# Two scores moved beside the attention outputs in a software-pipelined two-layer graph network

## The chip, the cores and the metric

The kernel runs on one core of a Trainium2 chip. Its time is device microseconds for one whole execution; a table entry is the median of several executions. The engines of the core are TensorE (PE in the profile: matmuls, and PEld: the loads of their weights), VectorE (DVE), ScalarE (ACT), GpSimd (POOL) and SyncE (SP, which here only issues DMAs). Each engine works through its own list of instructions strictly in order and waits on semaphores for the others.

## The reference

128 graphs of 128 nodes with 512 features pass two layers. Both start with a layer norm and a relu, and both add their result to x.

```python
# layer 0 (weights Wq, Wk, Wv of 512 x 512)
h = relu(layernorm(x))
q, k, v = h @ Wq.T, h @ Wk.T, h @ Wv.T
rel = adjacency.T * (q @ k.T)          # 128 x 128 for each graph
rel = rel / norm(rel, axis=2)
x = x + rel @ v
# layer 1 (8 heads of 64, with biases)
h = relu(layernorm(x))
q, k, v = h @ Wq + bq, h @ Wk + bk, h @ Wv + bv
scores = q @ k.T / sqrt(64) + (0 where adj else -1e9)
x = x + softmax(scores) @ v
```

All of it is float32.

## The kernel before

The 128 graphs are taken in 32 groups of four. A group passes four stages, and four neighbouring groups are in work at once. In the lists of steps their names are: `f`, the group whose x is being loaded and whose layer norm statistics are taken; `m`, the group in layer 0; `n`, the same group as `m` when its layer 1 starts (`n.stat`, `n.hn`, `n.T`); `l`, the group before, in layer 1; and `p`, the group before that, whose last two attention outputs and whose way back to x are still open. After a cycle each name passes on: `n` becomes `l`, `l` becomes `p`.

Every 512 x 512 product with a group's 512 rows is done in seven quarter products (steps `P1` to `P7`, a Strassen-Winograd scheme). Each is eight matmul passes of 128x256 in a PSUM bank, at line 218, followed by one emptying: a copy by ACT (`Q`, `K`, `G` and layer 0's `V`) or by DVE (layer 1's `V`, line 235), or an addition by DVE (line 242). Banks `x` and `z` are used by several of the seven in turn: `P1`, `P6`, `P7`, `P4` all accumulate in `x`, `P5` and `P3` in `z`. The next of them may not start before the emptying of the one before has read the bank: `Q.P6` waits for the copy of `Q.P1`, `Q.P3` for the copy of `Q.P5`, `Q.P7` for that of `Q.P6`, and `Q.P4` for the addition of `Q.P7`. There are four such banks, so `Q.P5` also waits for the addition of `Q.P2`, which gives a bank back and which needs the copy of `Q.P1`.

Matrices are turned with the help of DRAM. `hn`, `ex` and `oc` on ACT write a tile and send it to a scratch tensor (line 184, ACT's queue, one DMA of 512 KB); `rd`, `wr` and `rdo` fetch it back in blocks (line 192, SP's queue, four DMAs of 128 KB); `T`, `wt` and `ot` on DVE then transpose 32x32 blocks (lines 313, 478, 585). The fetched tiles share one pool of two buffers:

```python
tpool = ctx.enter_context(tc.tile_pool(name="tpool", bufs=2))
...
u = tpool.tile([P, n * TB, 8 * BK // n], F32, tag="u", name=f"u_{name}")
```

A fetch can't be issued before one of the two has been read by its transpose. In the program as built, for both kernels, the fetch `m.rd0` waits for `p.wt3`, and `m.rd1` for the second transpose of `p.ot0`.

Layer 1's attention of graph b is `S` (scores, line 445: 16 matmul passes with 64 rows and 128 columns of the array, eight heads into two PSUM banks of which there is one set), `mk` (DVE: mask added, line 454, and row maxima, line 456), `ex` (ACT: eight exponentials, line 463, and the send), `wr` (fetch), `wt` (DVE: reciprocal and transpose). `A0` and `A1` (line 562: 32 passes each, 128 rows and 64 columns) make the attention outputs of graphs 0, 1 and 2, 3. `oc`, `rdo`, `ot` bring them back: two ACT copies and a send, four fetches, and for each graph a transpose, a scaling (line 590, DVE), the addition to x and the store (lines 597 and 598, POOL).

The order of everything is written by hand, in four lists of steps: `FIRST`, `SECOND` (groups 0 and 1), `ORDER` (30 cycles) and `LAST`. The lists are emitted in turn under a manual schedule, so each engine's order is the order of the list, thinned to what that engine does; a step's instructions on all engines are emitted together. What a step on one engine waits for on another is worked out by the framework. DVE therefore does `p.wt3`, `p.ot0`, the addition of `Q.P3`, `m.T0`, the addition of `Q.P7`, `m.T1` in this sequence, in both kernels.

Of the kernel before, what the change touches and what calls it, by code (L numbers as in the profile page):

```python
# [21 lines left out]
def kernel(  # L22
# [343 lines left out]
    class Layer0(Layer):  # L366
        n = 0
# [54 lines left out]
    class Layer1(Layer):  # L422
        n = 1
# [189 lines left out]
        m.V.P2 l.S1 l.mk1 m.V.P5  # L613
        l.ex1 l.wr1 l.wt0 m.R m.mask_rel m.square f.stat2 f.stat3 f.inv1 m.V.P6 m.V.P3 m.N m.norms l.S2 l.mk2
        m.V.P7 l.ex2 l.wr2 l.wt1 m.O0 m.xO0 m.O1 m.xO1 n.stat0 n.stat1 n.inv0 m.V.P4 n.hn0 n.rd0 l.start_v l.V.P1
        m.O2 m.xO2 m.O3 m.xO3 n.stat2 n.stat3 n.inv1 l.S3 l.mk3 l.V.P2 l.V.P5 n.hn1 l.V.P6 l.wt2 n.rd1 l.ex3
        l.wr3 l.V.P3 l.V.P7 n.T0 l.A0 l.oc0 l.V.P4 n.T1 n.start
    """.split()
    ORDER = """
        l.Q.P1 p.rdo0 l.sumA l.Q.P2 m.hn0 l.sumB l.K.P1 m.rd0 m.hn1 l.K.P2 m.rd1 p.wt3 l.Q.P5  # L620
        p.ot0 l.Q.P6 l.Q.P3 p.A1 p.oc1 p.rdo1 m.T0 l.Q.P7 l.K.P5 m.T1 l.K.P6 l.Q.P4 f.load0 f.load1
        l.K.P3 m.sumA l.K.P7 m.sumB m.start m.G.P1 l.K.P4 m.G.P2 l.S0 l.mk0 m.G.P5 m.G.P6 l.ex0 l.wr0
        p.ot1 m.G.P3 m.V.P1 m.G.P7 f.stat0 f.stat1 f.inv0 m.V.P2 f.load2 f.load3 m.G.P4 l.S1 l.mk1 m.V.P5
        l.ex1 l.wr1 l.wt0 m.R m.mask_rel m.square f.stat2 f.stat3 f.inv1 m.V.P6 m.V.P3 m.N m.norms l.S2 l.mk2
        m.V.P7 l.ex2 l.wr2 l.wt1 m.O0 m.xO0 m.O1 m.xO1 n.stat0 n.stat1 n.inv0 m.V.P4 n.hn0 n.rd0 l.start_v l.V.P1
        m.O2 m.xO2 m.O3 m.xO3 n.stat2 n.stat3 n.inv1 l.S3 l.mk3 l.V.P2 l.V.P5 n.hn1 l.V.P6 l.wt2 n.rd1 l.ex3
        l.wr3 l.V.P3 l.V.P7 n.T0 l.A0 l.oc0 l.V.P4 n.T1 n.start
    """.split()
    LAST = """
        l.Q.P1 p.rdo0 l.sumA l.Q.P2 l.sumB l.K.P1 l.K.P2 p.wt3 l.Q.P5 p.ot0 l.Q.P6 l.Q.P3 l.K.P5 l.K.P6 l.K.P3  # L630
        l.Q.P7 l.S0 l.mk0 l.K.P7 l.Q.P4 l.ex0 l.wr0 l.K.P4 l.S1 l.mk1 p.A1 p.oc1 p.rdo1 l.start_v l.V.P1
        l.ex1 l.V.P2 l.V.P5 l.S2 l.mkA2 l.mkB2 l.V.P6 l.exA2 l.exB2 l.wt0 l.wr1 l.V.P3 l.V.P7 l.S3 l.mkA3 l.mkB3
        l.tw2 l.wt1 l.exA3 l.exB3 l.V.P4 l.An0 l.fin0 l.An1 l.fin1 p.ot1 l.tw3 l.An2 l.fin2 l.An3 l.fin3
# [15 lines left out]
    with tc.manual_schedule(engines={EN.PE, EN.SP, EN.Pool, EN.DVE, EN.Activation}):  # L649
        p, l, m = None, None, Layer0(0)  # L650
# [9 lines left out]
        f = Layer0(1)  # L660
# [7 lines left out]
        for g in range(NG):  # L668
            n = Layer1(g)
            if g:  # L670
                f = Layer0(g + 1) if g + 1 < NG else None
            run((FIRST, SECOND, ORDER)[min(g, 2)], p=p, l=l, m=m, n=n, f=f, w=Weights1())
            p, l, m = l, n, f
# [31 lines left out]
```

## Time and profile before

| | |
|---|---|
| median of 3 runs | 2538.28 us (2534.71 to 2539.89) |
| the profiled execution's own time | 2538.26 us |
| its span, first to last instruction | 2536.5 us |
| PE busy | 2512.7 us (99%) |
| DVE, ACT, POOL busy | 1707.5 (67%), 1023.9 (40%), 535.0 us (21%) |
| one of the 30 cycles, by the repeat of the same matmul | 77.57 us |
| granted TensorE clock, mean | 0.997 |

A busy share is the engine's own; matmuls overlap each other, so PE's share is not a share of its peak. The chain that ended last follows the work back from the last instruction, at each step to what released it. In a view by time, a line gives start and duration in us, the engine (q: its queue), the line of the kernel, the operation, out<-in, the shapes, how many instructions were merged, and in square brackets the idle time before it and what ended it. The scratch tensors are `d_h`, `d_w`, `d_o`; what is fetched from them is `u_h`, `u_w`, `u_o`.

### The profile page before, as it was taken

The page shows a single profiled execution, that of the slowest core. Times are in us where ns is not written, and L with a number is a line of the kernel's source. Part 1 is how long each engine was busy: PE and PEld are TensorE (multiplying, and loading weights), DVE is VectorE, ACT ScalarE, POOL GpSimd, SP SyncE. Part 2 cuts the span into 40 slices and gives each one's busy share as a digit, 9 for nine tenths or more (in the row PEclk, how much of TensorE's full clock was granted, in tenths as well). Part 3 has the DMA queues.
Part 4 walks back from the last instruction along what each step waited for, and adds up shares of the span by engine and source line. Part 5 has one row for each costly group of instructions (what it writes and reads, how often), then busy time and mean ns, then how long its engine had stood idle before and what let it go on. Part 6 is the DMA issues. An engine that isn't in the chain of part 4 may idle for free.

```text
span 2536.5 us, 40820 instructions
## 1 busy us (share of the span) xinstructions
PE 2512.7 (99%) x14672; PEld 2135.8 (84%) x14672; DVE 1707.5 (67%) x2484; ACT 1023.9 (40%) x3248; POOL 535.0 (21%) x945
## 2 busy tenths in 40 slices
PE   8999999999999999999999999999999999999998
PEld 6888888888888888888888888888888888888886
DVE  5566766667676667666677666676666676666765
ACT  2334443444433344434444333444344443334433
POOL 5121212211122212121111222121211112221211
PEclk9999999999999999999999999999999999999999
DMA  5255544555444555445554445554455644455542
GB/s 171 88 179 166 187 145 140 172 170 185 154 145 151 182 167 183 146 146 168 168 188 152 142 155 178 171 182 142 148 169 165 193 151 143 156 176 174 175 133 93
DMA packets 370475, 405.71 MB, mean 160 GB/s; under 512 B 29600, under 2 KB 286752, under 8 KB 370272
## 3 DMA queue, kind: packets, MB, share of 16 engines
q1 hardware_dynamic: 278992, 167.92, 23.4%
q10 hardware_dynamic: 70384, 166.74, 17.8%
q0 software_dynamic: 20896, 68.44, 7.8%
q8 instruction: 115, 1.88, 0.3%
q14 instruction: 88, 0.72, 0.1%
HBM read 204.80 MB, written 198.18 MB: 159 GB/s over the span
## 4 chain that ended last, share of the span: by engine, by line
PE 97%; DVE 1%; DMA 1%; ACT 0%; issue 0%; POOL 0%; SPq 0%; ACTq 0%; DVEq 0%; POOLq 0%
PE pv_x L218 18%; PE pq_x L218 9%; PE pv_z L218 9%; PE pk_x L218 9%; PE pg_x L218 8%; PE pss L445 5%; PE po L562 5%; PE pv_y L218 5%; PE pg_z L218 4%; PE pq_z L218 4%; PE pr L382 4%; PE pk_z L218 4%; PE po L414 4%; PE pk_y L218 2%; PE pg_y L218 2%; PE pq_y L218 2%
## 5 line engine op out<-in xcount | busy, mean ns | idle before, releaser
L463 ACT ACTIVATE e<-pss,nmax 128x128 f32<-128x128 f32 x1008 | 355.0, 380 | 190.9 <-DVE nmax L456 168.5
L597 POOL TENSOR_TENSOR xb<-xb,o 128x512 f32<-128x512 f32 x124 | 158.2, 1276 | 1103.6 <-DVE o L590 976.4
L218 PE MATMUL pv_x<-wc_v,h 128*128 128x256 f32 x1280 | 300.8, 382 | 0.0
L218 PEld LDWEIGHTS pv_x<-wc_v,h 128*128 128x128 f32 x1280 | 240.3, 190 | 51.0 <-DVE v L242 11.7
L301 ACT ACTIVATE hn<-xb,shift,rstd 128x512 f32<-128x512 f32 x252 | 190.9, 807 | 152.4 <-POOL shift L293 152.4
L218 PE MATMUL pv_z<-wc_v,s 128*128 128x256 f32 x1024 | 245.1, 382 | 0.0
L313 DVE STREAM_TRANSPOSE h<-u_h 128x1024 f32<-128x1024 f32 x126 | 156.5, 1242 | 98.9 <-DMA u_h<-d_h 92.0
L463 ACT ACTIVATION_READ_ACCUMULATOR e<-pss,nmax 128x1 f32 x1008 | 221.2, 219 | 0.0
L454 DVE TENSOR_TENSOR pss<-pss,mask 128x1024 f32<-128x1024 f32 x126 | 154.7, 1228 | 96.2 <-PE pss L445 96.2
L218 PEld LDWEIGHTS pv_z<-wc_v,s 128*128 128x128 f32 x1024 | 192.0, 190 | 28.6
L218 PE MATMUL pv_x<-wc_v,s 128*128 128x256 f32 x768 | 184.9, 384 | 0.0
L218 PE MATMUL pq_x<-h,wc_q 128*128 128x256 f32 x768 | 184.7, 383 | 0.0
L283 DVE BATCH_NORM_STATS2 st<-xb 128x6 f32<-128x512 f32 x256 | 172.0, 672 | 16.6 <-DMA xb<-in_x_dram 16.6
L218 PE MATMUL pk_x<-h,wc_k 128*128 128x256 f32 x768 | 181.5, 379 | 0.0
L445 PEld LDWEIGHTS pss<-kT,qT 64*128 64x128 f32 x2048 | 124.6, 188 | 48.7 <-PE po L414 23.5
L290 POOL TENSOR_SCALAR rstd<-mv 128x2 f32<-128x2 f32 x128 | 28.6, 223 | 642.8 <-DVE mv L284 642.7
L218 PEld LDWEIGHTS pq_x<-h,wc_q 128*128 128x128 f32 x768 | 143.4, 190 | 23.5 <-ACT oT L573 5.1
L218 PEld LDWEIGHTS pk_x<-h,wc_k 128*128 128x128 f32 x768 | 145.8, 190 | 19.9
L218 PEld LDWEIGHTS pv_x<-wc_v,s 128*128 128x128 f32 x768 | 140.8, 190 | 20.4
L456 DVE TENSOR_REDUCE nmax<-pss 128x8 f32<-128x1024 f32 x126 | 154.2, 1224 | 4.4
L478 DVE STREAM_TRANSPOSE wT<-u_w 128x1024 f32<-128x1024 f32 x126 | 150.3, 1193 | 3.6 <-DMA u_w<-d_w 3.6
L445 PE MATMUL pss<-kT,qT 64*128 64x128 f32 x2048 | 149.2, 285 | 2.7 <-ACT e L463 2.3
(147 smaller groups left out, 4460.2 us busy)
## 6 DMA issues: line engine op xcount, KB each, us to landing
d_h<-hn ACTq DMA_DIRECT2D x126, 512.0 KB, 3.5
u_h<-d_h SPq DMA_DIRECT2D x504, 128.0 KB, 3.3
d_w<-e ACTq DMA_DIRECT2D x126, 512.0 KB, 2.6
u_w<-d_w SPq DMA_DIRECT2D x504, 128.0 KB, 2.9
xb<-in_x_dram POOLq DMA_DIRECT2D x124, 256.0 KB, 3.2
d_o<-oT ACTq DMA_DIRECT2D x62, 512.0 KB, 4.1
u_o<-d_o SPq DMA_DIRECT2D x248, 128.0 KB, 3.1
out_dram<-xb POOLq DMA_DIRECT2D x124, 256.0 KB, 2.8
```

What stands on the lines that cost most here:

```text
L218: nc.tensor.matmul(ps[:, m, :], lhsT=lhsT, rhs=rhs, start=first and m == 0 and k == 0, stop=k == 1, skip_group_check=True,)
L283: nc.vector.bn_stats(st, x_tiles[g, b])
L301: nc.scalar.activation(hn[:, r], x_tiles[g, b].rearrange("p (k j q) -> p j k q", j=TB, q=BK), AF.Relu, bias=self.shift[:, b : b + 1], scal ...
L313: nc.vector.transpose(half.rearrange("p k (t i) -> p t k i", i=BK), self.u.pop(i).rearrange("p t (k q) -> p t k q", q=BK),)
L382: nc.tensor.matmul(pr[:, b, :], lhsT=self.turned(k, b), rhs=self.gT[:, k, ts(b, P)], start=(k == 0), stop=(k == KD - 1),)
L445: nc.tensor.matmul(pss[:, r, k, :], lhsT=self.qT[rows, k, ts(b, P)], rhs=self.kT[rows, k, ts(b, P)], start=True, stop=True,)
L454: nc.vector.tensor_tensor(sc, sc, mask[:, None, :].to_broadcast([P, H, P]), ALU.add)
L456: nc.vector.tensor_reduce(self.nmax[b], sc, AX.X, ALU.max, negate=True)
L463: nc.scalar.activation(e[:, :, i, :], sc[:, i, :].rearrange("p (j q) -> p j q", q=BK), AF.Exp, bias=nmax[:, i : i + 1], accum_out=self.tot ...
L478: nc.vector.transpose(self.wT[b].rearrange("p h (t i) -> p t h i", i=BK), self.uw.pop(b).rearrange("p t (h q) -> p t h q", q=BK),)
L562: nc.tensor.matmul(po[r * HD : (r + 1) * HD, k, :], lhsT=self.v[:, b, ts(2 * k + r, HD)], rhs=wT[:, r * NH + k, :], start=True, stop=True,)
L597: nc.gpsimd.tensor_tensor(xb, xb, o.rearrange("p k t q -> p (k t q)"), ALU.add)
```

## The change

Only the lists of steps change, and no computation. In `SECOND` and `ORDER`, `l.S3` with `l.mk3` and `l.ex3` goes from behind `m.xO3` to the end of the cycle: `S3` stands directly before `A0`, `mk3` after it and behind `n.T0`, `ex3` after `oc0`. Its fetch, `wr3`, is now made in the next cycle, as `p.wr3` behind `p.rdo0` and `Q.P2` (also in `LAST`). In `ORDER`, `p.A1` goes from behind `Q.P3` to directly behind `l.S0`; `p.oc1` and `p.rdo1` follow it there, and `p.ot1` goes behind `m.G.P7`. `f.load2` and `f.load3` go from behind `m.V.P2` to behind `l.wr1`, and `f.stat2 f.stat3 f.inv1` from behind `m.square` to behind `n.hn1`.

```diff
     ORDER = """
-        l.Q.P1 p.rdo0 l.sumA l.Q.P2 m.hn0 l.sumB l.K.P1 m.rd0 m.hn1 l.K.P2 m.rd1 p.wt3 l.Q.P5
-        p.ot0 l.Q.P6 l.Q.P3 p.A1 p.oc1 p.rdo1 m.T0 l.Q.P7 l.K.P5 m.T1 l.K.P6 l.Q.P4 f.load0 f.load1
-        l.K.P3 m.sumA l.K.P7 m.sumB m.start m.G.P1 l.K.P4 m.G.P2 l.S0 l.mk0 m.G.P5 m.G.P6 l.ex0 l.wr0
-        p.ot1 m.G.P3 m.V.P1 m.G.P7 f.stat0 f.stat1 f.inv0 m.V.P2 f.load2 f.load3 m.G.P4 l.S1 l.mk1 m.V.P5
-        l.ex1 l.wr1 l.wt0 m.R m.mask_rel m.square f.stat2 f.stat3 f.inv1 m.V.P6 m.V.P3 m.N m.norms l.S2 l.mk2
+        l.Q.P1 p.rdo0 l.sumA l.Q.P2 p.wr3 m.hn0 l.sumB l.K.P1 m.rd0 m.hn1 l.K.P2 m.rd1 p.wt3 l.Q.P5
+        p.ot0 l.Q.P6 l.Q.P3 m.T0 l.Q.P7 l.K.P5 m.T1 l.K.P6 l.Q.P4 f.load0 f.load1
+        l.K.P3 m.sumA l.K.P7 m.sumB m.start m.G.P1 l.K.P4 m.G.P2 l.S0 p.A1 l.mk0 p.oc1 p.rdo1 m.G.P5 m.G.P6
+        l.ex0 l.wr0 m.G.P3 m.V.P1 m.G.P7 p.ot1 m.V.P2 f.stat0 f.stat1 f.inv0 m.G.P4 l.S1 l.mk1 m.V.P5
+        l.ex1 l.wt0 l.wr1 f.load2 f.load3 m.R m.mask_rel m.square m.V.P6 m.V.P3 m.N m.norms l.S2 l.mk2
         m.V.P7 l.ex2 l.wr2 l.wt1 m.O0 m.xO0 m.O1 m.xO1 n.stat0 n.stat1 n.inv0 m.V.P4 n.hn0 n.rd0 l.start_v l.V.P1
-        m.O2 m.xO2 m.O3 m.xO3 n.stat2 n.stat3 n.inv1 l.S3 l.mk3 l.V.P2 l.V.P5 n.hn1 l.V.P6 l.wt2 n.rd1 l.ex3
-        l.wr3 l.V.P3 l.V.P7 n.T0 l.A0 l.oc0 l.V.P4 n.T1 n.start
+        m.O2 m.xO2 m.O3 m.xO3 n.stat2 n.stat3 n.inv1 l.V.P2 l.V.P5 n.hn1 f.stat2 f.stat3 f.inv1 l.V.P6 l.wt2
+        n.rd1 l.V.P3 l.V.P7 n.T0 l.S3 l.A0 l.mk3 l.oc0 l.V.P4 l.ex3 n.T1 n.start
     """.split()
```

The last two lines of `SECOND` change in the same way as those of `ORDER`, without the steps of `f`, and `LAST` gains `p.wr3` behind `l.Q.P2`.

More of the change, by code (lines that the diff above doesn't have):

```diff
@@ L615 @@
         m.V.P7 l.ex2 l.wr2 l.wt1 m.O0 m.xO0 m.O1 m.xO1 n.stat0 n.stat1 n.inv0 m.V.P4 n.hn0 n.rd0 l.start_v l.V.P1
-        m.O2 m.xO2 m.O3 m.xO3 n.stat2 n.stat3 n.inv1 l.S3 l.mk3 l.V.P2 l.V.P5 n.hn1 l.V.P6 l.wt2 n.rd1 l.ex3
-        l.wr3 l.V.P3 l.V.P7 n.T0 l.A0 l.oc0 l.V.P4 n.T1 n.start
+        m.O2 m.xO2 m.O3 m.xO3 n.stat2 n.stat3 n.inv1 l.V.P2 l.V.P5 n.hn1 l.V.P6 l.wt2
+        n.rd1 l.V.P3 l.V.P7 n.T0 l.S3 l.A0 l.mk3 l.oc0 l.V.P4 l.ex3 n.T1 n.start
     """.split()
     ORDER = """
-        l.Q.P1 p.rdo0 l.sumA l.Q.P2 m.hn0 l.sumB l.K.P1 m.rd0 m.hn1 l.K.P2 m.rd1 p.wt3 l.Q.P5
-        p.ot0 l.Q.P6 l.Q.P3 p.A1 p.oc1 p.rdo1 m.T0 l.Q.P7 l.K.P5 m.T1 l.K.P6 l.Q.P4 f.load0 f.load1
-        l.K.P3 m.sumA l.K.P7 m.sumB m.start m.G.P1 l.K.P4 m.G.P2 l.S0 l.mk0 m.G.P5 m.G.P6 l.ex0 l.wr0
-        p.ot1 m.G.P3 m.V.P1 m.G.P7 f.stat0 f.stat1 f.inv0 m.V.P2 f.load2 f.load3 m.G.P4 l.S1 l.mk1 m.V.P5
-        l.ex1 l.wr1 l.wt0 m.R m.mask_rel m.square f.stat2 f.stat3 f.inv1 m.V.P6 m.V.P3 m.N m.norms l.S2 l.mk2
+        l.Q.P1 p.rdo0 l.sumA l.Q.P2 p.wr3 m.hn0 l.sumB l.K.P1 m.rd0 m.hn1 l.K.P2 m.rd1 p.wt3 l.Q.P5
[3 more added lines that the diff above has]
+        l.ex1 l.wt0 l.wr1 f.load2 f.load3 m.R m.mask_rel m.square m.V.P6 m.V.P3 m.N m.norms l.S2 l.mk2
         m.V.P7 l.ex2 l.wr2 l.wt1 m.O0 m.xO0 m.O1 m.xO1 n.stat0 n.stat1 n.inv0 m.V.P4 n.hn0 n.rd0 l.start_v l.V.P1
-        m.O2 m.xO2 m.O3 m.xO3 n.stat2 n.stat3 n.inv1 l.S3 l.mk3 l.V.P2 l.V.P5 n.hn1 l.V.P6 l.wt2 n.rd1 l.ex3
-        l.wr3 l.V.P3 l.V.P7 n.T0 l.A0 l.oc0 l.V.P4 n.T1 n.start
+        m.O2 m.xO2 m.O3 m.xO3 n.stat2 n.stat3 n.inv1 l.V.P2 l.V.P5 n.hn1 f.stat2 f.stat3 f.inv1 l.V.P6 l.wt2
+        n.rd1 l.V.P3 l.V.P7 n.T0 l.S3 l.A0 l.mk3 l.oc0 l.V.P4 l.ex3 n.T1 n.start
     """.split()
     LAST = """
-        l.Q.P1 p.rdo0 l.sumA l.Q.P2 l.sumB l.K.P1 l.K.P2 p.wt3 l.Q.P5 p.ot0 l.Q.P6 l.Q.P3 l.K.P5 l.K.P6 l.K.P3
+        l.Q.P1 p.rdo0 l.sumA l.Q.P2 p.wr3 l.sumB l.K.P1 l.K.P2 p.wt3 l.Q.P5 p.ot0 l.Q.P6 l.Q.P3 l.K.P5 l.K.P6 l.K.P3
         l.Q.P7 l.S0 l.mk0 l.K.P7 l.Q.P4 l.ex0 l.wr0 l.K.P4 l.S1 l.mk1 p.A1 p.oc1 p.rdo1 l.start_v l.V.P1
```

## The prediction

> **What bounds the kernel now.** I read the page first: busy shares and the chain that ended last.
>
> ```profile
> PE 2512.7 (99%) x14672; PEld 2135.8 (84%) x14672; DVE 1707.5 (67%) x2484; ACT 1023.9 (40%) x3248; POOL 535.0 (21%) x945
> ...
> PE 97%; DVE 1%; DMA 1%; ACT 0%; issue 0%; POOL 0%; SPq 0%; ACTq 0%; DVEq 0%; POOLq 0%
> ```
>
> TensorE is the chain. From one cycle to the next the same matmul comes 77.57 us later, and between two matmuls inside a cycle there is no wait, only what a change of shape costs. So a cycle gets shorter only by less PE work or cheaper changes of shape, and any new wait of PE is paid in full. Next, PE by time around the moved score:
>
> ```profile
> 1057.60 1.88 PE L414 MATMUL po<-v,rel 128*128 128x512 f32 x4
> 1059.40 1.16 PE L445 MATMUL pss<-kT,qT 64*128 64x128 f32 x16
> 1060.50 1.99 PE L218 MATMUL pv_y<-wc_v,h 128*128 128x256 f32 x8
> 1062.33 1.89 PE L218 MATMUL pv_z<-wc_v,s 128*128 128x256 f32 x8
> ...
> 1067.51 1.89 PE L218 MATMUL pv_x<-wc_v,h 128*128 128x256 f32 x8
> 1069.33 1.97 PE L562 MATMUL po<-wT,v 128*64 128x128 f32 x32
> 1071.22 1.99 PE L218 MATMUL pv_x<-wc_v,h 128*128 128x256 f32 x8
> 1073.06 1.89 PE L218 MATMUL pq_x<-h,wc_q 128*128 128x256 f32 x8
> ```
>
> The reader should take starts from starts. A quarter product takes 1.727 (1062.33 to 1064.05 and on). The one after S3 takes 1.83, the one before A0 1.82. Then the two engines that the moved steps join, DVE first:
>
> ```profile
> 1071.10 1.25 DVE L313 STREAM_TRANSPOSE h<-u_h 128x1024 f32<-128x1024 f32 x1 [0.97 <-DMA u_h<-d_h]
> ...
> 1080.95 1.19 DVE L478 STREAM_TRANSPOSE wT<-u_w 128x1024 f32<-128x1024 f32 x1
> ...
> 1088.06 1.25 DVE L313 STREAM_TRANSPOSE h<-u_h 128x1024 f32<-128x1024 f32 x1 [1.14 <-DMA u_h<-d_h]
> 1089.23 0.65 DVE L242 TENSOR_TENSOR qT<-pq_x,pq_r 128x512 f32<-128x512 f32 x1
> ```
>
> These are n.T0, p.wt3, m.T0 and the addition of Q.P7. Both T0 wait for a fetch, and the addition is queued behind the second. ACT, with ex3, then the copies of Q.P1, K.P1, Q.P5:
>
> ```profile
> 1065.65 0.37 ACT L463 ACTIVATE e<-pss,nmax 128x128 f32<-128x128 f32 x1 [0.53 <-DVE pv_r L235]
> ...
> 1068.59 0.34 ACTq L184 DMA_DIRECT2D d_w<-e  x1
> ...
> 1074.98 0.84 ACT L229 ACTIVATE pq_r<-pq_x,bq_sb 128x256 f32<-128x256 f32 x2 [3.06 <-PE pq_x L218]
> ...
> 1078.44 0.84 ACT L229 ACTIVATE pk_r<-pk_x,bk_sb 128x256 f32<-128x256 f32 x2 [1.21 <-DVE s L360]
> ...
> 1081.89 0.84 ACT L229 ACTIVATE pq_r<-pq_z,bq_sb 128x256 f32<-128x256 f32 x2 [1.21 <-PE pq_z L218]
> ```
>
> ACT idles 3.06 before the first copy. Last, how long a DMA takes to land, and SP's own waits:
>
> ```profile
> u_h<-d_h SPq DMA_DIRECT2D x504, 128.0 KB, 3.3
> d_w<-e ACTq DMA_DIRECT2D x126, 512.0 KB, 2.6
> u_w<-d_w SPq DMA_DIRECT2D x504, 128.0 KB, 2.9
> ```
>
> ```profile
> SPq L192 <- DVE wT L478: 33.6, 31, 3.6
> ```
>
> Once a cycle (31 times) SP waits for wt3 before it can fetch for m.T0: that is the two-buffer pool, already binding.
>
> **The change part by part: the gain.** Two changes of shape go. Alone, S3 costs: entry 1.80 less four passes of 0.43 = 0.09; 1.10 less eight pairs of 0.111 = 0.21; the slow product behind it 0.10; together 0.40. A alone: 0.09, 1.89 less 16 pairs of 0.109 = 0.15, and 1.84 less 1.727 = 0.11; together 0.35. Joined, S's exit (half of its 0.21, and the slow product: 0.20) and A's entry (0.09 and 0.05 of its 0.15: 0.14) are replaced by a change from S to A. That stands once in the trace, in LAST, at half clock: 0.35 from the last score to the first output where 0.20 is usual, and 0.05 more behind it, so 0.20; 0.10 if it scales with the clock. A join saves 0.34 - 0.20 = 0.14 to 0.34 - 0.10 = 0.24; if the change from S to A cost nothing, 0.34. I take 0.24, since every pitch there is about doubled. Sixty-one joins (two in 30 cycles, one in SECOND): -14.6 us, bounds -8.5 and -21.
>
> [...]
>
> **The chain that gets longer.** I follow S3 through the new order in the times of this cycle.
> 1. n.T0 ends at 1071.10 + 1.25 = 1072.34, set by a DMA that does not move. S3 is done by 1069.2, but mk3 now stands behind T0 on DVE: 2.49 (its two rows 1.21 and 1.22 with gaps), to 1074.86. Before, it ended at 1064.26.
> 2. ex3: first exponential to the start of its send 1068.59 - 1065.65 = 2.94; send starts 1077.83; ACT is free at 1078.21.
> 3. ACT's next is the copy of Q.P1: 1078.21, not 1074.98. From a copy over hn and its send to the next copy it is 2.70, so K.P1's copy comes at 1080.91 and Q.P5's at 1083.61, ending 1084.45.
> 4. The planned PE: Q.P1 at 1072.85 (1073.06 less a join), each product 1.727 later. Q.P5 (planned 1079.76) waits for the addition of Q.P2, hence Q.P1's copy (1079.05 + 0.75): 0.1 late. Q.P3 (planned 1083.3) waits for Q.P5's copy until 1084.5: 1.2 late. Each wait adds 0.10 for a slow first matmul.
> 5. wr3: the send lands after a; SP issues four (1.30 from first to last), the last lands after b; wt3 takes 1.30; only then m.rd0 is issued (1.34 from first to last) and lands after c; m.T0 1.25 and the addition of Q.P7 0.67. With 0.25 of semaphores: Q.P4 can start at 1077.83 + a + 1.30 + b + 1.30 + 1.34 + c + 1.92 + 0.25 = 1083.94 + a + b + c. Landings in the trace: a 2.6 to 3.75, b 2.9 to 4.0, c 2.7 to 4.2. The least sum is 8.2, the greatest 11.95. I take a = 2.6, b = 3.9 (a send of hn runs beside it; the fetch at 1059 beside such a send took 3.9 to 4.2), c = 2.8 (nothing else runs): 9.3, so 1093.2.
> 6. Q.P4 is planned at 1072.85 + 10 x 1.727 = 1090.1. It is 3.1 late, with the slow first matmul 3.2; the 1.4 of step 4 lie inside this. Least 2.1, greatest 5.8.
>
> The loop closes through PE: T0's DMA hangs on layer 0's outputs of the same cycle, which come after the late Q.P4. So every cycle pays: -0.48 + 3.2 = +2.7, times 30 = +82 us; bounds +1.6 and +5.3: +48 and +159.
>
> **The other moved pieces.** A1 and oc1 leave the stretch behind Q.P3 (they gave it 2.1 us of air, already counted as absent in the plan) and stand behind S0; mk0 now waits for A1's end, and ex0 still follows G.P6's copy: nothing. rdo1's four fetches pass to SP before wr0, when SP waited for d_w anyway: nothing. p.ot1 (3.4 on DVE) lies before V.P2's addition; d_o 4.1 + 1.3 + u_o 3.1 behind oc1 bring it just when G.P7's addition is done. mk1, ex1 and the square shift by about 1.7 and leave N half a microsecond; a landing as slow as that of u_o at 1015 (up to 5.3) would cost 1.5 a cycle, which stays for the upper range. load2 and load3 on POOL then wait for the stores of ot1, five microseconds before rn needs POOL, and their statistics (1.69 on DVE) run in the gap that mk3 leaves at 1062; V.P7 then has 0.3 left. POOL's f.inv1 follows n.inv1: nothing. FIRST and LAST stay, within 1 us.
>
> **The clock.** PE waited 2.00 in LAST before S1, and the clock fell to half for the next window:
>
> ```profile
> 2494.20:2497.60 3.40, 1.40 (x13) 0.95 (x13) 0.00 (x0) 2.93 (x18) 0.00 (x0) 1.00 0.01 2
> 2497.60:2501.00 3.40, 3.40 (x34) 3.18 (x34) 2.13 (x2) 1.06 (x3) 0.00 (x0) 0.50 0.43 163
> ```
>
> A wait of 1.22 at 43 us did not do it. The new waits are 1.2 and about 1.8, so in between; a half window costs 3.4 / 2 = 1.7 us. [...] I put nothing in the sum and +51 us (30 x 1.7) into a rival.
>
> **The rivals.** (a) Faster: no chain closes, only the joins count, 2523.7. It needs T0's fetch to land some 2 us sooner, so that mk3 starts at 1070 and the landings are at their least; then ACT also catches up. For it: sends and fetches at 1058 to 1074 land slowly (u_h 4.0) and ex3's own traffic leaves that stretch. Against: T0's fetch is issued at 1065.4, before that traffic began. It decides from a chain 2.7 us shorter on. (b) Only ACT's queue binds: a, b, c small or the pool laxer, stalls 1.4 - 0.48 = +0.9 a cycle: 2565. (c) The clock falls in each cycle: 2538.3 + 82 + 51 = 2671. (d) The change does nothing: excluded by the moved lines, but gain and loss could cancel at a stall of 0.48.
>
> **How the numbers follow.** The profiled execution took 2538.26, its span 2536.5, the median of the runs is 2538.28: the sum stands against either. Likeliest, 0.62: 2538.3 + 82 = 2620, own range 2586 to 2697. (b) 0.12, (c) 0.13, (a) 0.11, (d) 0.02. The range leaves out (a) and little above: 2556 to 2697. About 0.2% can be told from no change: faster 0.11, same 0.02, slower 0.87.
>
> **What would show it.** In the profile after: PE idle before pq_z (Q.P3) released by ACT pq_r, and before pq_x (Q.P4) released by DVE qT, once a cycle; the copy of Q.P1 following d_w's send without idle time; SP waiting for wt3 much longer; score and output starts 0.15 to 0.3 us closer than now, with a cycle near 80.3. A cycle of 77.1 without idle time on PE would make the prediction wrong, and so would a T0 that begins before 1070 in this cycle's times.

## The result, and the profile after

The changed kernel takes 2653.35 us (median of six runs, 2645.68 to 2667.78) where the kernel before takes 2538.07 (2534.71 to 2539.89): 1.0461 times as long, interval 1.043 to 1.0491. It is slower by 115 us. The profiled execution of the changed kernel took 2660.64 us, its span is 2658.9, so it lies 7 above the median; sums below are made against 2660.64 - 2538.26 = 122.4. A cycle takes 81.55 us on average (77.57 before); the shortest takes 79.05.

The page, busy shares and the chain that ended last:

```profile
PE 2550.7 (96%) x14672; PEld 2160.7 (81%) x14672; DVE 1703.2 (64%) x2484; ACT 1018.8 (38%) x3248; POOL 535.9 (20%) x945
...
PE 57%; DMA 17%; DVE 13%; SPq 5%; ACT 4%; issue 3%; POOL 1%; DVEq 0%; ACTq 0%; POOLq 0%
```

PE was 97% of the chain and is now 57%: a path through DMAs, DVE, ACT and SP's queue carries the rest. Where PE's matmuls wait (us in total, times, longest):

```profile
PE pq_x L218 <- DVE qT L242: 71.6, 30, 4.2
PE pq_z L218 <- ACT pq_r L229: 10.7, 17, 1.0
```

The first line is `Q.P4` waiting for the addition of `Q.P7`, once a cycle; the second is `Q.P3` waiting for the copy of `Q.P5`. These are the two places that the prediction named. One cycle of PE by time, from the product before the joined `S3` and `A0` to `Q.P4`:

```profile
1031.34 1.89 PE L218 MATMUL pv_x<-wc_v,h 128*128 128x256 f32 x8
1033.16 1.16 PE L445 MATMUL pss<-kT,qT 64*128 64x128 f32 x16
1034.25 1.97 PE L562 MATMUL po<-wT,v 128*64 128x128 f32 x32
1036.15 1.99 PE L218 MATMUL pv_x<-wc_v,h 128*128 128x256 f32 x8
...
1046.61 1.89 PE L218 MATMUL pq_x<-s,wc_q 128*128 128x256 f32 x8
1048.89 1.99 PE L218 MATMUL pq_z<-s,wc_q 128*128 128x256 f32 x8 [0.40 <-ACT pq_r L229]
...
1054.18 1.89 PE L218 MATMUL pk_x<-s,wc_k 128*128 128x256 f32 x8
1058.93 3.16 PE L218 MATMUL pq_x<-h,wc_q 128*128 128x256 f32 x8 [2.86 <-DVE qT L242]
1061.88 2.45 PE L218 MATMUL pk_z<-s,wc_k 128*128 128x256 f32 x8
```

The score and the output stand 1.09 us apart. `Q.P6` to `Q.P3` is 2.28 where a product takes 1.727: 0.55 late. `K.P6` to `Q.P4` is 4.75, so `Q.P4` is 3.02 late, and it then takes 2.95 to the next start: half clock. The other two engines in the same cycle, DVE first (`n.T0`, the two rows of `mk3`, `p.wt3`, the addition of `Q.P3`, `m.T0`, the addition of `Q.P7`):

```profile
1035.65 1.25 DVE L313 STREAM_TRANSPOSE h<-u_h 128x1024 f32<-128x1024 f32 x1 [1.69 <-DMA u_h<-d_h]
1036.82 1.20 DVE L454 TENSOR_TENSOR pss<-pss,mask 128x1024 f32<-128x1024 f32 x1
1038.05 1.22 DVE L456 TENSOR_REDUCE nmax<-pss 128x8 f32<-128x1024 f32 x1
...
1051.85 1.25 DVE L478 STREAM_TRANSPOSE wT<-u_w 128x1024 f32<-128x1024 f32 x1 [4.86 <-DMA u_w<-d_w]
...
1056.29 0.68 DVE L242 TENSOR_TENSOR qT<-pq_z,pq_r 128x512 f32<-128x512 f32 x1
1057.06 1.25 DVE L313 STREAM_TRANSPOSE h<-u_h 128x1024 f32<-128x1024 f32 x1
1058.22 0.65 DVE L242 TENSOR_TENSOR qT<-pq_x,pq_r 128x512 f32<-128x512 f32 x1
```

ACT, from the first exponential of `ex3` to its send and the copies of `Q.P1`, `K.P1` and `Q.P5`:

```profile
1039.31 0.37 ACT L463 ACTIVATE e<-pss,nmax 128x128 f32<-128x128 f32 x1 [2.46 <-DVE nmax L456]
...
1042.25 0.34 ACTq L184 DMA_DIRECT2D d_w<-e  x1
1042.63 0.84 ACT L229 ACTIVATE pq_r<-pq_x,bq_sb 128x256 f32<-128x256 f32 x2 [0.42 <-ACT e L463]
...
1045.32 0.84 ACT L229 ACTIVATE pk_r<-pk_x,bk_sb 128x256 f32<-128x256 f32 x2 [0.45 <-PE pk_y L218]
...
1048.00 0.84 ACT L229 ACTIVATE pq_r<-pq_z,bq_sb 128x256 f32<-128x256 f32 x2 [0.44 <-ACT hn L301]
```

Before, ACT idled 3.06 us ahead of the copy of `Q.P1`; now that copy stands directly behind the send of `ex3`. The chain in order of time (start, us, what) shows the way round in this cycle:

```profile
1042.25 3.42 DMA d_w<-e
...
1047.41 4.32 DMA u_w<-d_w
...
1051.85 1.26 DVE wT L478
1053.10 0.02 issue
1053.12 0.30 SPq L192
...
1054.45 2.58 DMA u_h<-d_h
...
1058.93 3.16 PE pq_x L218 x8
```

The fetch for `m.T0` is issued 0.02 us after `wt3` has ended: SP was waiting for that pool buffer. In SP's own waits the line for `wt3` was 33.6 us before and there was none for the landing of `u_w`. Now there are both:

```profile
SPq L192 <- DMA u_w<-d_w: 88.3, 53, 4.0
SPq L192 <- DVE wT L478: 40.6, 31, 3.3
```

Together 128.9 us: in each cycle SP stands first until the fetch `wr3` has landed, then until its transpose is done, and 40.6 / 31 = 1.31 us is the length of that transpose.

Last, the clock over the wait before `Q.P4` (by stretches; us, busy time of PE, PEld, DVE, ACT, POOL with instructions, then granted clock, DMA share, GB/s):

```profile
1056.20:1059.60 3.40, 0.67 (x3) 0.62 (x4) 2.59 (x4) 0.75 (x2) 2.40 (x3) 1.00 0.83 256
1059.60:1063.00 3.40, 3.40 (x10) 2.66 (x9) 1.25 (x1) 0.84 (x2) 1.09 (x2) 0.50 0.62 171
1063.00:1066.40 3.40, 3.40 (x17) 2.98 (x17) 1.92 (x4) 0.00 (x0) 0.00 (x0) 1.00 0.12 46
```

One stretch of 3.4 us at half speed follows the stretch in which PE was idle: 10 passes where 17 are usual. The profile has 24 stretches at half speed (one in the cycles is two windows of 3.4 us long), that of before 3. Of the 30 waits before `Q.P4`, 21 are followed by one.

### The profile page after: what moved, and what is told of

It is laid out like the page before. It is cut to its first block, busy times and chain, and to the rows that moved or that the text cites. A ratio compares the mean times of both kernels' runs of the same rounds, so it can differ in the third digit from the quotient of the medians.

```text
span 2658.9 us, 40753 instructions
## 1 busy us (share of the span) xinstructions
PE 2550.7 (96%) x14672; PEld 2160.7 (81%) x14672; DVE 1703.2 (64%) x2484; ACT 1018.8 (38%) x3248; POOL 535.9 (20%) x945
## 4 chain that ended last, share of the span: by engine, by line
PE 57%; DMA 17%; DVE 13%; SPq 5%; ACT 4%; issue 3%; POOL 1%; DVEq 0%; ACTq 0%; POOLq 0%
PE pv_x L218 9%; PE pg_x L218 8%; DMA u_h<-d_h 7%; PE pv_z L218 6%; DMA u_w<-d_w 5%; SPq L192 5%; PE pk_x L218 4%; PE pg_z L218 4%; PE pq_x L218 4%; PE pr L382 4%; PE pss L445 4%; ACT e L463 4%; DMA d_w<-e 3%; PE pv_y L218 3%; PE po L414 3%; DVE h L313 3%
## 5 line engine op out<-in xcount | busy, mean ns | idle before, releaser
L218 PE MATMUL pq_x<-h,wc_q 128*128 128x256 f32 x768 | 213.4, 427 | 71.6 <-DVE qT L242 71.6
L218 PEld LDWEIGHTS pq_x<-h,wc_q 128*128 128x128 f32 x768 | 160.3, 213 | 108.6 <-DVE qT L242 83.7
L573 ACT COPY oT<-po 128x512 f32<-128x512 f32 x124 | 72.7, 586 | 265.9 <-PE po L562 265.9
```

The lines of the kernel that those rows point to most:

```text
L218: nc.tensor.matmul(ps[:, m, :], lhsT=lhsT, rhs=rhs, start=first and m == 0 and k == 0, stop=k == 1, skip_group_check=True,)
```

## The experiments

Theory: the way round through `mk3`, `ex3`, the send, the fetch `wr3`, `wt3`, the pool buffer and the fetch for `m.T0` has become longer than the PE work between `S3` and `Q.P4`, and PE pays the difference. Rivals: ACT's queue alone costs the time; the other moved pieces (`A1`, `oc1`, `rdo1`, `ot1`, the loads and statistics) cost it; the half clock costs it. The edits below are shown against the changed kernel, and `...` stands for lines left out. Runs sent together share the runs of the kernel before, at 2539.23 us for four of them (`e2_maxima_first`, `e3_only_S0_A1`, `e4_only_S3_A0`, `e7_exponential_later`) and 2537.04 us for the others.

### Each half of the change alone

The change joins two pairs. In one the score `S3` moves to the output `A0`; in the other it is the output `A1` that moves, to the score `S0`. First `S0` and `A1` joined, all of `S3` where it was before. In the first form the statistics moved too, as in the change:

```diff
-        m.O2 m.xO2 m.O3 m.xO3 n.stat2 n.stat3 n.inv1 l.V.P2 l.V.P5 n.hn1 f.stat2 f.stat3 f.inv1 l.V.P6 l.wt2
-        n.rd1 l.V.P3 l.V.P7 n.T0 l.S3 l.A0 l.mk3 l.oc0 l.V.P4 l.ex3 n.T1 n.start
+        m.O2 m.xO2 m.O3 m.xO3 n.stat2 n.stat3 n.inv1 l.S3 l.mk3 l.V.P2 l.V.P5 n.hn1 f.stat2 f.stat3 f.inv1 l.V.P6 l.wt2 n.rd1 l.ex3
+        l.wr3 l.V.P3 l.V.P7 n.T0 l.A0 l.oc0 l.V.P4 n.T1 n.start
...
```

> Only one of the two joins: A1 with oc1, rdo1, ot1 and the loads of the half group move as in the change, S3, mk3, ex3 and wr3 stay where they were before. Theory: nothing of the loop is lengthened, so only the join shows: 30 cycles by 0.24, 2531 us (2526 to 2536), a cycle of 77.33. Rival (the loss comes from this half of the change): 2600 to 2650, with PE waiting behind V.P2, at N or at Q.P4.

Measured: 2550.82, 1.0047 (1.0033 to 1.006). That missed. The loss has a line of its own among the waits:

```profile
PEld pv_x L218 <- DVE pv_r L235: 15.0, 30, 0.6
```

`V.P7` waits for DVE in every cycle: the statistics (1.69 us on DVE) and `mk3` now stand in the same stretch. The prediction had costed the statistics at nothing because `mk3` left that stretch, which holds for the whole change and not for this half. So the second form leaves the loads and statistics of the next group where they were:

```diff
-        l.ex0 l.wr0 m.G.P3 m.V.P1 m.G.P7 p.ot1 m.V.P2 f.stat0 f.stat1 f.inv0 m.G.P4 l.S1 l.mk1 m.V.P5
-        l.ex1 l.wt0 l.wr1 f.load2 f.load3 m.R m.mask_rel m.square m.V.P6 m.V.P3 m.N m.norms l.S2 l.mk2
+        l.ex0 l.wr0 m.G.P3 m.V.P1 m.G.P7 p.ot1 m.V.P2 f.load2 f.load3 f.stat0 f.stat1 f.inv0 m.G.P4 l.S1 l.mk1 m.V.P5
+        l.ex1 l.wt0 l.wr1 m.R m.mask_rel m.square f.stat2 f.stat3 f.inv1 m.V.P6 m.V.P3 m.N m.norms l.S2 l.mk2
...
```

> The S0 and A1 join alone, once more, with the two statistics of the half group where the kernel before has them, behind m.square, and their loads ahead of f.inv0 so that they have landed. In the first form the statistics stood between two emptyings of layer 1's V together with mk3, and PE waited 0.27 and a slow first matmul before V.P7 in each cycle. Theory: without that the join's 0.20 shows, 30 cycles, 2533 us (2528 to 2538). Rival (moving A1, oc1, rdo1 and ot1 costs by itself): 2545 to 2555 as before.

Measured: 2535.76, 0.9992 (0.9984 to 1.0001): the interval just touches no change. The median cycle is 77.37, so one join saves 77.57 - 77.37 = 0.20 us and `A1`, `oc1`, `rdo1` and `ot1` cost nothing where they stand; a few waits in single cycles (1.3 us in five of them before a product of `V` in bank `z`, 1.3 in two before `Q.P4`, the slow first passes behind them) raise the average of the thirty cycles to 77.51 and take 4 of the 6 us back.

The other half: `S3`, `mk3`, `ex3` and `wr3` moved, `A1` and the rest as before.

```diff
-        p.ot0 l.Q.P6 l.Q.P3 m.T0 l.Q.P7 l.K.P5 m.T1 l.K.P6 l.Q.P4 f.load0 f.load1
+        p.ot0 l.Q.P6 l.Q.P3 p.A1 p.oc1 p.rdo1 m.T0 l.Q.P7 l.K.P5 m.T1 l.K.P6 l.Q.P4 f.load0 f.load1
...
```

> Only the other join: S3, mk3, ex3 and wr3 move as in the change, A1, oc1, rdo1, ot1 and the loads stay where they were before. Theory: the loop is as long as in the changed kernel, A1 gives PE 2.1 us more work before Q.P4, but A1 needs wt3 itself (about 1087.3 in the times of the prediction, planned 1085.0). So PE waits at A1 for DVE's wT, 2 to 3 us a cycle, and little or nothing at Q.P4: 2590 to 2640 with the half clock that such waits bring. Rival (this half is harmless): 2531.

Measured: 2579.21, 1.0163 (1.0149 to 1.0177), eleven below the expected range, a cycle of 78.96. The waits of the weight loads:

```profile
PEld pq_x L218 <- DVE qT L242: 20.0, 20, 2.8
PEld po L562 <- DVE wT L478: 17.7, 24, 2.0
```

`A1` itself waits for `wt3` here, and `Q.P4` waits less. Counted from the first pass of `O2`, `Q.P4` starts at 36.20 (35.72 in the changed kernel), but by then PE has also done `A1`, 2.1 us of work. That is why the two halves don't add up: about -1 and +40 alone, +115 together. Taking `A1` away from behind `Q.P3` costs nothing by itself, but that is the stretch in which PE now waits, and `A1` had been filling it. The waits here are shorter, and no half window falls into the cycles (granted clock 0.998 on average), where the changed kernel has 22 (0.983): some 36 of the 82.7 us between the two profiled executions (2660.64 and 2577.99).

### The front of the way round: maxima before the transpose

`mk3` needs `S3`, and `n.T0` a fetch that lands later. Here `S3` and `A0` stand before `n.T0`, in `SECOND` and `ORDER`.

```diff
-        n.rd1 l.V.P3 l.V.P7 n.T0 l.S3 l.A0 l.mk3 l.oc0 l.V.P4 l.ex3 n.T1 n.start
+        n.rd1 l.V.P3 l.V.P7 l.S3 l.A0 l.mk3 n.T0 l.oc0 l.V.P4 l.ex3 n.T1 n.start
```

> The changed kernel with S3, A0 and mk3 ahead of n.T0 instead of behind it; nothing else moves. Theory (the loop mk3, ex3, wr3, wt3, m.rd0, m.T0, Q.P7's addition, Q.P4): mk3 then starts when S3 is done (1069.2 in the times of the prediction) and not when T0 ends (1072.34), so ex3 and all behind it comes 3.1 us sooner in each cycle, and the waits before Q.P3 and Q.P4 shrink from some 3 us to a few tenths; T0 itself ends 0.6 later, which Q.P1 just about bears. About 2532 us (2522 to 2550). Rival (the loss comes from A1, oc1, rdo1 and ot1, now between S0 and V.P2): T0 and mk3 do not matter, about 2650. Rival (the late exponentials only fill ACT's queue, and the fetch of m.T0 is slow for its own reasons): the wait before Q.P3 goes, the one before Q.P4 stays, 2600 to 2640.

Measured: 2592.99, 1.0209 (1.0189 to 1.0228): 60 us better than the changed kernel, 60 worse than expected. `mk3` ends 2.3 us sooner (14.17 after `O2` instead of 16.45), but `ex3` begins only 1.8 sooner because it now queues behind `oc0` on ACT, and `Q.P4` starts 1.45 sooner (34.27). With the shorter waits, five half windows are left in the cycles where the changed kernel has 22 (granted clock 0.995 on average, 0.983 there). DVE by time shows where the rest stays:

```profile
1027.15 1.25 DVE L478 STREAM_TRANSPOSE wT<-u_w 128x1024 f32<-128x1024 f32 x1 [3.00 <-DMA u_w<-d_w]
...
1031.60 0.68 DVE L242 TENSOR_TENSOR qT<-pq_z,pq_r 128x512 f32<-128x512 f32 x1
1032.42 1.25 DVE L313 STREAM_TRANSPOSE h<-u_h 128x1024 f32<-128x1024 f32 x1
```

Behind `wt3` stand the four steps of `ot0` and the addition of `Q.P3`; in this cycle `m.T0` follows them almost at once, but on average over 26 cycles DVE idles 0.59 us before `m.T0`, in 23 of them until its fetch has landed. So from `wt3` to `m.T0` two ways are about equally long: DVE's queue (4.0 us) and the fetch through the pool (4.5 on average here, 4.4 in the changed kernel, where it is 4.0 in the cycle shown, 1053.10 to 1057.06). Whoever wants `m.T0` sooner has to move `wt3`, not only what stands before it.

### The back of the way round: the fetch and its transpose later

`ex3` stays as in the change. `wr3` goes behind `m.T0` and `wt3` behind `m.sumB`, so that `m.rd0` no longer waits for `wt3`, and `ot0`, the addition of `Q.P3` and `m.T0` no longer stand behind it on DVE.

```diff
-        l.Q.P1 p.rdo0 l.sumA l.Q.P2 p.wr3 m.hn0 l.sumB l.K.P1 m.rd0 m.hn1 l.K.P2 m.rd1 p.wt3 l.Q.P5
-        p.ot0 l.Q.P6 l.Q.P3 m.T0 l.Q.P7 l.K.P5 m.T1 l.K.P6 l.Q.P4 f.load0 f.load1
-        l.K.P3 m.sumA l.K.P7 m.sumB m.start m.G.P1 l.K.P4 m.G.P2 l.S0 p.A1 l.mk0 p.oc1 p.rdo1 m.G.P5 m.G.P6
+        l.Q.P1 p.rdo0 l.sumA l.Q.P2 m.hn0 l.sumB l.K.P1 m.rd0 m.hn1 l.K.P2 m.rd1 l.Q.P5
+        p.ot0 l.Q.P6 l.Q.P3 m.T0 p.wr3 l.Q.P7 l.K.P5 m.T1 l.K.P6 l.Q.P4 f.load0 f.load1
+        l.K.P3 m.sumA l.K.P7 m.sumB p.wt3 m.start m.G.P1 l.K.P4 m.G.P2 l.S0 p.A1 l.mk0 p.oc1 p.rdo1 m.G.P5 m.G.P6
```

> The changed kernel with wr3 behind m.T0 and wt3 behind m.sumB; ex3 stays where the change has it, ahead of the copy of Q.P1. So m.rd0 waits for n.T1 and not for wt3, and neither ot0 nor m.T0 stands behind wt3 on DVE, while ACT's queue is as in the changed kernel. Theory (the loop through the fetches is the cost before Q.P4, ACT's queue only the few tenths before Q.P3): the wait before Q.P4 goes and with it the half clock; the wait before Q.P3 stays at 0.4 to 0.6 a cycle; 2526 + 15 = 2541 us (2530 to 2555). Rival (the late exponentials alone hold everything up through ACT): the wait before Q.P4 stays, 2600 or more.

Measured: 2542.76, 1.002 (1.0011 to 1.0029), a cycle of 77.61. Of the 115 us, 110 are gone with two steps moved on SP and DVE and nothing changed on PE or ACT. What remains stands mostly before `Q.P3`, behind ACT's queue:

```profile
PE pq_z L218 <- ACT pq_r L229: 5.7, 10, 0.9
PE pq_x L218 <- DVE qT L242: 3.3, 5, 0.8
```

So the way from the fetch `wr3` on is the cause, and the rival "only ACT's queue" is worth half a microsecond a cycle: 15 us against the run with both joins and no such wait (2527.8, the last run of the next part). This run lifts two holds at once, the pool buffer and the place of `wt3` in DVE's queue, and no run parts them. The trace of the changed kernel does in part: `m.T0` starts 4.44 us behind the end of `wt3` on average and 3.96 at the least, which is what DVE's steps in between take. So the pool holds `m.T0` up by some 0.5 us more than DVE's queue alone would. With the long wait the half clock has gone from the cycles too: the granted clock is 0.997 on average, as before, where the changed kernel has 0.983.

### The whole way round later

First `ex3` too, behind `Q.P6`, with `wr3` behind `m.T0` and `wt3` behind `K.P6`:

```diff
-        l.Q.P1 p.rdo0 l.sumA l.Q.P2 p.wr3 m.hn0 l.sumB l.K.P1 m.rd0 m.hn1 l.K.P2 m.rd1 p.wt3 l.Q.P5
-        p.ot0 l.Q.P6 l.Q.P3 m.T0 l.Q.P7 l.K.P5 m.T1 l.K.P6 l.Q.P4 f.load0 f.load1
+        l.Q.P1 p.rdo0 l.sumA l.Q.P2 m.hn0 l.sumB l.K.P1 m.rd0 m.hn1 l.K.P2 m.rd1 l.Q.P5
+        p.ot0 l.Q.P6 p.ex3 l.Q.P3 m.T0 p.wr3 l.Q.P7 l.K.P5 m.T1 l.K.P6 p.wt3 l.Q.P4 f.load0 f.load1
...
```

> Both joins as in the change, and mk3 behind T0 as in the change, but what hangs on mk3 moves to where nothing waits for it: ex3 behind Q.P6 of the next cycle (ACT idle there since A1 and oc1 left), wr3 behind m.T0, wt3 behind K.P6; A1 behind S0 is its only user. m.rd0 then waits for n.T1 and m.rd1 for ot0, not for wt3. Theory: no wait of PE is left, both joins are kept: 61 joins by 0.24 (bounds 0.14 and 0.34), 2524 us (2517 to 2530), a cycle of 77.1. Rival (A1, oc1, rdo1 and ot1 behind S0 cost something themselves): above 2538, with PE waiting between S0 and S2.

Measured: 2679.24, 1.056 (1.0545 to 1.0575), a cycle of 82.3: worse than the change itself. `Q.P4` no longer waits, but `K.P4` does:

```profile
1069.84 1.89 PE L218 MATMUL pg_x<-h,wc_a 128*128 128x256 f32 x8
1074.62 3.50 PE L218 MATMUL pk_x<-h,wc_k 128*128 128x256 f32 x8 [2.90 <-DVE kT L242]
```

```profile
1070.83 1.25 DVE L478 STREAM_TRANSPOSE wT<-u_w 128x1024 f32<-128x1024 f32 x1 [5.69 <-DMA u_w<-d_w]
1072.00 0.65 DVE L242 TENSOR_TENSOR kT<-pk_z,pk_r 128x512 f32<-128x512 f32 x1
...
1073.88 0.69 DVE L242 TENSOR_TENSOR kT<-pk_x,pk_r 128x512 f32<-128x512 f32 x1
```

`wt3` stands on DVE for 5.69 us waiting for its fetch, and the additions of `K.P3` and `K.P7` stand behind it, though their inputs are there. The wait had only been moved to the next product that shares DVE's queue, and 32 half windows fall into the cycles (22 in the changed kernel; granted clock 0.977 on average, 0.983 there). With `wt3` some steps further, behind `m.sumB`, nothing that PE needs soon stands behind it:

```diff
...
-        p.ot0 l.Q.P6 l.Q.P3 m.T0 l.Q.P7 l.K.P5 m.T1 l.K.P6 l.Q.P4 f.load0 f.load1
-        l.K.P3 m.sumA l.K.P7 m.sumB m.start m.G.P1 l.K.P4 m.G.P2 l.S0 p.A1 l.mk0 p.oc1 p.rdo1 m.G.P5 m.G.P6
+        p.ot0 l.Q.P6 p.ex3 l.Q.P3 m.T0 p.wr3 l.Q.P7 l.K.P5 m.T1 l.K.P6 l.Q.P4 f.load0 f.load1
+        l.K.P3 m.sumA l.K.P7 m.sumB p.wt3 m.start m.G.P1 l.K.P4 m.G.P2 l.S0 p.A1 l.mk0 p.oc1 p.rdo1 m.G.P5 m.G.P6
...
```

> As the run with ex3 behind Q.P6 and wr3 behind m.T0, but wt3 goes from behind K.P6 to behind m.sumB. In that run PE waited 3.4 us a cycle before K.P4 for the addition of K.P7, which stood on DVE behind wt3, and wt3 stood there until its fetch had landed. Theory (any transpose that waits for a fetch holds up the additions behind it on DVE): behind sumB nothing that PE needs soon stands behind wt3; A1, its user, comes 3 us after it. No wait of PE is left, both joins are kept at the 0.20 that the changed kernel's profile shows for one: 61 x 0.20 = 12 us, 2526 us (2520 to 2532), a cycle of 77.17. Rival (A1, oc1, rdo1 and ot1 behind S0 cost something of their own): above 2538.

Measured: 2527.8 (2524.78 to 2529.25), 0.9962 (0.9949 to 0.9974): faster than both kernels. The cycle is 77.18 in nearly every repeat, 0.39 below before: two joins at 0.20. Page, the chain that ended last:

```profile
PE 96%; DVE 1%; DMA 1%; issue 1%; ACT 1%; POOL 0%; SPq 0%; DVEq 0%; POOLq 0%; ACTq 0%
```

This is the time that the joins alone are worth, with the same matmuls in the same order as in the change, and it shows that the whole loss of the change came from where `ex3`, `wr3` and `wt3` stood.

### Filling the wait

The changed kernel with one more step, `l.fill`, behind `K.P6`: eight matmul passes (1.73 us) into a bank that nobody reads. The outputs are computed as before; PE does 30 x 1.73 = 52 us more.

```diff
+        def fill(self):
+
+            idle = ps_o.tile([P, 2, HF], F32, tag="po", name=f"idle_{self.g}")
+            for m in range(2):
+                for k in range(2):
+                    nc.tensor.matmul(
+                        idle[:, m, :], lhsT=wc["q"][:, W11, k, ts(m, P)], rhs=self.x11[:, k, :],
+                        start=m == 0 and k == 0, stop=k == 1, skip_group_check=True,
+                    )
...
-        p.ot0 l.Q.P6 l.Q.P3 m.T0 l.Q.P7 l.K.P5 m.T1 l.K.P6 l.Q.P4 f.load0 f.load1
+        p.ot0 l.Q.P6 l.Q.P3 m.T0 l.Q.P7 l.K.P5 m.T1 l.K.P6 l.fill l.Q.P4 f.load0 f.load1
```

> The changed kernel with eight more matmul passes (1.73 us) ahead of Q.P4, into a bank that nobody reads: they wait for nothing and give PE something to do while it waits there. Theory (Q.P4's time is set by the loop, so work ahead of it is free, and what the loop does not explain of the loss is the half clock after idle time): the wait shrinks from 2.5 to 0.8 us, the half clock stays away in nearly all cycles, a cycle becomes the 79.9 that the undisturbed cycles of the changed kernel show, 2610 us (2600 to 2625), some 40 us faster with 52 us more work. Rival (PE's own work is the bound, or the half clock comes from something else): 2650 to 2705.

Measured: 2611.14 (2609.04 to 2612.47), 1.029 (1.0274 to 1.0306): 42 us faster than the changed kernel, with more work. Its waits before `Q.P4`:

```profile
PE pq_x L218 <- DVE qT L242: 8.6, 11, 2.2
```

The cycle is 79.95 on average, with one half window in all thirty, where the changed kernel has 81.55 and 22 (granted clock 0.996 on average, 0.983 there). So the way round sets when `Q.P4` starts, and work put into the wait is free. Most of the 1.6 us a cycle between the two kernels is the clock (1.2, worked out below). The rest is that `Q.P4` starts a little sooner here, 35.21 behind the first pass of `O2` where the changed kernel has 35.72; why, no run shows.

## Why the prediction was right or wrong

Slower was right; 2620 was forecast, 2653.35 measured, within the range (2556 to 2697) and 33 above the forecast. By its own steps:

**The gain of a join.** 0.24 taken, bounds 0.14 and 0.34. Measured 0.20 (`e3b_only_S0_A1` and half of the 0.39 of `e8_all_later`). From the last score to the first output the changed kernel takes 202 ns in every cycle where 105 is usual, so the change from S to A does cost something, and 0.34 is out. 61 x 0.20 = 12.2 us instead of 14.6.

**The way round, steps 1 to 3.** Here the order of events was right and two sizes were off in opposite directions. Times from the first pass of `O2`, means over 26 cycles (a, b and c: from issue to landing):

| event | predicted | measured |
|---|---|---|
| `n.T0` starts | 13.50 | 12.82 |
| `mk3` ends | 17.26 | 16.45 |
| send of `ex3` starts | 20.23 | 19.42 |
| the send of `ex3` (term a) | 2.6 | 3.35 |
| slowest of the four fetches of `u_w` (term b) | 3.9 | 3.9 |
| slowest of the four fetches for `m.T0` (term c) | 2.8 | 2.96 |
| `Q.P4` starts | 35.64 | 35.72 |

The cycle from which step 1 took `n.T0` was a late one (the kernel before has 12.81 on average too); it starts 0.7 sooner, and that was given back by the landing of the send, which took 0.75 longer. That both errors cancel is luck, and step 5 came out within 0.1 us by it. The bounds of a, b and c were too narrow: over the cycles of the kernel before, single landings take 2.6 to 4.9, 2.4 to 6.2 and 2.2 to 6.8. And the sign that a `T0` before 1070 would make the prediction wrong was too strict: in 7 of the 26 cycles `n.T0` starts before 12.40, which is 1070 in the prediction's times, and `Q.P4` waits in these too.

**Step 4, the step that failed: how the delay is shared between two waits.** It made `Q.P3` 1.2 us late, so that only 1.8 of the 3.2 were left to wait before `Q.P4`. As `ex3` began 0.8 us sooner than step 2 had it, ACT's queue was that much earlier, and `Q.P3` waited 0.44 on average (0 to 1.14). The total hardly changed: the waits before `Q.P4` sum to 76.5 us, those before `Q.P3` to 13.9, and 49 slow first matmuls at 0.10 make 4.9, together 95 where 30 x 3.2 = 96 was forecast. But the wait before `Q.P4` is now 2.5 us on average, not 1.8.

**The clock, the term that was mis-sized.** It stood at nothing in the sum and at +51 in rival (c), on the ground that a wait of 1.22 had not brought it down, 2.00 had, and 1.8 lay between. With 2.5 most waits lie above, and a half window came in 21 of 30 cycles, in one of them two. In these 22 windows of 3.41 us PE waited 3.5 us anyway, so they cost (22 x 3.41 - 3.5) / 2 = 36 us, where the kernel before has none in its cycles. That is nearly the whole miss: -12 + 95 + 36 = 119 of the 122.4 of the profiled execution; the other 3 I have not assigned. The forecast of 80.3 for a cycle stands beside 81.55 less 36 / 30, which is 80.35. (The cycles without a half window take 79.94 and those with one 82.27, but their waits before `Q.P4` differ too, 2.0 and 2.8 on average.) So the likeliest case and rival (c) were one case, which the wait decides cycle by cycle by its length and, as the last section shows, by when it falls; and (c) with 2671 was nearer than its chance of 0.13 said.

**The other moved pieces** were put at nothing: confirmed by `e3b_only_S0_A1` and `e8_all_later`, with the exception that `e3_only_S0_A1` shows how thin it is (with `mk3` in the same stretch the moved statistics cost 13 us). What the prediction did not see is that `A1` had covered the stretch where the new wait arises. It counted the absent 2.1 us in the plan of PE, rightly for the total; but that this made the two halves of the change cost far more together than apart was not said.

**Rivals.** (a) needed a chain 2.7 us shorter; it was not shorter at all. (b), ACT's queue alone, is refuted by `e5b_fetch_later`: 2542.76 with the queue as in the change, where (b) had 2565. (d) fell with the loss.

## What to carry to other kernels

Before a piece of work is moved behind a round trip through DRAM, follow the trip to its end: what buffer does its fetch hold, which fetch of another group waits for that buffer, and what stands behind its transpose in its engine's queue, as two additions did on DVE in `e7_exponential_later` while `wt3` waited 5.69 us. (Which of the last two costs more was not parted here.) A later consumer, not an earlier producer, mended it here: moving the fetch and its transpose behind what PE needs next gave back 110 of 115 us, and moving the transpose not far enough was worse than not at all. And when one change takes work out of a stretch and another puts a wait there, price the two together, with the length of each single wait and not only their sum, since half speed followed single windows of 3.41 us with about 2.0 us of idle time or more here.

## What the runs showed of the hardware

**Half speed fell on a grid of 3.413 us here, behind single windows with about 2.0 us of idle time or more.** All 24 stretches at half speed in the profile of the changed kernel begin whole multiples of 3.413 us from each other. I laid PE's idle time (from 0.24 us after the start of the last pass to the start of the next) onto that grid. Leaving out the first 100 us and the end of the matmuls, 22 windows at full speed (21 in the cycles, one in `LAST`) hold 2.01 to 3.33 us of idle time and are followed by a half window; of the others none holds more than 1.92, except one with 2.07. One window that was itself at half speed (from 2121 us) was followed by a second: it held 1.54 us of idle time (here from 0.46 us after a pass's start, as passes stand 0.43 apart), and the other 22 at half speed at most 0.52. The last stretch begins 0.94 us behind the last matmul, after a window with 0.97 us of idle time, so the 2.0 is shown for waits between matmuls only. A wait cost some 1.7 us (half of 3.41) or nothing in this profile, as it fell within a window or across two: a wait of 2.04 within one window (before 407 us) brought a half window, and one of 2.24 that was cut into 1.92 and 0.33 (before 1958 us) brought none.

**More matmuls made the changed kernel faster.** Eight unread passes in each wait, 52 us in all, took 42 us off the changed kernel (2653.35 to 2611.14); some 36 of its time had been half speed, and one half window of 22 is left in the cycles.

**A change between the two tiled shapes cost about what one from full to tiled did.** 64x128 to 128x64 added 0.10 us between the two passes in the changed kernel (202 ns where 105 is usual) and some 0.05 behind them (154 ns where 103 is usual); full to 128x64 added 0.09 in the kernel before (309 ns where 216 is usual) and the same 0.05.
